# A selective scan over two images: image 0 reads its states out by C products summed in pairs, image 1 keeps transposed states

## The chip, the core and the metric

The kernel runs on one core of a Trainium2 chip. The metric is the device time of one execution in microseconds; before the change, seven executions have a median of 7278.53 us (7260.23 to 7296.72). Engine names are those of the profile: PE is TensorE (PEld its weight loads), DVE is VectorE, ACT is ScalarE, POOL is GpSimd, SP is SyncE, which here only issues DMAs.

## What is computed

The program is a two-layer network on 2 images of 128 channels and 64 x 64 positions, in float32. Layer 0 is a deformable convolution with four branches and a mixture of 8 experts; layer 1 is a Mamba-like mixer and a second mixture of experts. The change is in the mixer's selective scan, for 256 channels `d` (two halves of 128 partitions), 16 states `n` and 4096 positions `l` of each image:

```python
dA = jnp.exp(jnp.einsum('bdl,dn->lbdn', delta, A))
dBu = jnp.einsum('bdl,bnl,bdl->lbdn', delta, Bm, x)
def step(s, inp):
    a, bu, c = inp
    s = a * s + bu
    return (s, jnp.einsum('bdn,bn->bd', s, c))
_, ys = lax.scan(step, jnp.zeros((b, DI, DS), x.dtype), (dA, dBu, Ct))
y = jnp.transpose(ys, (1, 2, 0)) + x * D[None, :, None]
out = jnp.einsum('md,bdl->blm', out_proj_w, y * silu(z))
```

Per state the values of all positions are one recurrence; the readout multiplies state `n` by row `n` of C and sums over the 16 states.

## The kernel before

**Stages.** Up to about 5448 us the deformable convolution of both images runs, paced by gathers on POOL; beside image 1's sampling, image 0 goes through the rest of layer 0 and the mixer's convolutions. From 5448 to 7020 us the scan runs: image 0 first, then image 1. Beside image 0's scan the program does image 1's remaining work (`after(1)`: fusing the branches, L842 to L899; the experts' groups, `L0Ffn.group`; the mixer's convolutions, `L1Conv.convs`). Beside image 1's scan there is nothing but the scan's own preparation. After 7020 us comes the last mixture of experts.

**Units.** `L1Conv.scan` cuts each image into 8 chunks of 512 positions. A chunk has 32 units, one for each half and state; a unit is one recurrence over 128 partitions and 512 positions, so there are 256 units per image. The order of instructions on every engine is the order in which this Python loop emits them; each engine runs its own queue in order and waits on semaphores. For unit `u` the loop emits:

- SP: the B row of a unit six ahead (`fetch`, L1598), read from DRAM and spread over 128 partitions (tile `bcb`, 8 buffers).
- DVE: the scan of `u` (L1668): `h = da * state + db` from PSUM tile `da` and SBUF tile `db` into SBUF tile `h` (3 buffers).
- POOL: `db` of `u+3` (`drive`, L1580; 4 buffers), and the copy of the last column of `h` of `u-1` into `state` for the next chunk (L1677).
- ACT: `da` of `u+2`, an exponential into PSUM (`decay`, L1587; 2 buffers).
- PE: four 128 x 128 transposes of `h` of `u-1` into PSUM tile `ht` (`turn`, by the helper on L120; 2 buffers), so that positions lie on partitions and C is a scalar for each partition.
- DVE and ACT: `weigh` of `u-2`: C times `ht` into SBUF tile `w`. For image 0, DVE takes two of the four 128-column blocks in one instruction (L1614) and ACT the other two (L1616); for image 1, DVE one and ACT three.
- PE: four transposes of `w` of `u-3` back, accumulated over the 16 states in PSUM tile `py` (`add`, L1625), which an identity-like product with D (L1622) has started. After the 16th state, DVE multiplies `py` into the gate `zc` (L1637), and `project` multiplies by the output weights (L1710).

Between units the loop takes two steps of `prepare` (the next chunk: convolution taps, `x_proj`, `delta`, `du`; L1470 to L1548) and steps of `after(1)` worth one unit of credit, so how much of the other work stands beside each unit is fixed by the program.

**PSUM.** Eight banks: `da` 2, `ht` 2, `py` 1, and 3 (`scm`) for everything else.

Of the kernel before, what the change touches and what calls it, by code (L numbers as in the profile page):

```python
# [10 lines left out]
F32 = mybir.dt.float32  # L11
I32 = mybir.dt.int32
AF = mybir.ActivationFunctionType
ALU = mybir.AluOpType
# [5 lines left out]
P = 128  # L20
B = 2
C = 128
# [3 lines left out]
GT = 4  # L26
# [14 lines left out]
DS = 16  # L41
LC = 512
# [168 lines left out]
class L0Conv:  # L211
# [690 lines left out]
    def residual(self, b, g, keep, sp):  # L902

        nc, cut = self.env.nc, slice(g * 512, (g + 1) * 512)
        row = lambda name: sp.tile([P, 512], F32, name=name, tag="t", bufs=7)
        xr, fa, fn = row("xr"), row("fa"), row("fn")
        nc.sync.dma_start(out=xr, in_=self.env.d["x"][b, :, cut])
        nc.sync.dma_start(out=fa, in_=self.fd[b][:, cut])
        for _ in range(3):
            yield  # L910
        for py in range(2):
            nat = view(fn, py * W, [(2 * W, 4), (2, 32), (1, 2)])
            phases = view(fa, py * 256, [(32, 4), (1, 32), (P, 2)])
            nc.scalar.activation(nat, phases, AF.Relu, bias=keep[:, 1:2], scale=keep[:, 0:1])
        yield
        yield
        return xr, fn


class L0Ffn:  # L920
# [26 lines left out]
    def group(self, b, g, residual, norm, x2, sp, pp):  # L947
        env, nc = self.env, self.env.nc
        bank = lambda shape, name: pp.tile(shape, F32, name=name, tag="m")
        row = lambda name: sp.tile([P, GT, C], F32, name=name, tag="t", bufs=7)  # L950
        act = b > 0
        parts = yield from residual(b, g, sp)
        yield from self.take()
        pt = bank([P, GT, P], "pt")
# [127 lines left out]
AHEAD = 3  # L1082
BCB = 8

# [30 lines left out]
class L1Conv:  # L1115
# [315 lines left out]
    def taps(self, b, k, xc, xs, zz, sa, sp, bank, wk):  # L1431

        env, nc, halves = self.env, self.env.nc, range(2)
        if k == 0:
            self.wd = self.room().tile([P, 2, 4, P], F32, name="wd")
            for h in halves:
                for t in range(4):
                    nc.scalar.mul(self.wd[:, h, t, :], env.ident, self.w1[b][:, h, t : t + 1])
                yield
# [27 lines left out]
    def prepare(self, b, k, sp, pp, res):  # L1467
# [13 lines left out]
        def gap(n):  # L1481
            for _ in range(n):
                yield

        yield from gap(11)
        zz = sp.tile([P, 2, LC], F32, name="zc")
        nc.sync.dma_start(out=zz, in_=self.zsd[b].rearrange("(h p) l -> p h l", p=P)[:, :, l0 : l0 + LC])
# [3 lines left out]
        halves = range(2)  # L1491
        xs = sp.tile([P, 2, LC], F32, name="xs")
        if b:
            yield from self.taps(b, k, xc, xs, zz, sa, sp, bank, wk)
        else:
            yield from self.tap_sums(b, xc, xs, zz, sa, wk)
# [6 lines left out]
        nc.scalar.copy(xd, px)  # L1503
        bc = self.dp.tile([DS, LC], F32, name=f"bc{b}_{k}", tag=f"bc{b}_{k}")
        nc.sync.dma_start(out=bc, in_=xd[8 : 8 + DS, :])
        res.update(bc=bc)
        yield
        pt = bank([P, GT, 40], "pt")
        for j in range(GT):
            nc.tensor.transpose(pt[:, j, :], xd[:, j * P : (j + 1) * P], env.ident[0:40, 0:40])  # L1510
        yield
        ct = sp.tile([P, GT, DS], F32, name="ct")
        nc.scalar.copy(ct, pt[:, :, 8 + DS :])
        res.update(ct=ct)
        v = wk("v")
# [35 lines left out]
    def scan(self, sp, ps, pp, rest, ahead):  # L1551
# [18 lines left out]
        for _ in gen:  # L1570
            pass
        units = [(k, half, n) for k in range(B * NK) for half in range(2) for n in range(DS)]
        pieces, das, dbs, rows, hs, hts, ws = {0: res}, {}, {}, {}, {}, {}, {}

        def drive(u):

            if u < len(units):
                k, half, n = units[u]
                dbs[u] = sp.tile([P, LC], F32, name="db", bufs=AHEAD + 1)
                nc.gpsimd.tensor_tensor(dbs[u], pieces[k]["du"][:, half, :], rows.pop(u), ALU.mult)  # L1580

        def decay(u):
            if u < len(units):
                k, half, n = units[u]
                das[u] = ps.tile([P, LC], F32, name="da")
                dl = pieces[k]["dl"][:, half, :]
                nc.scalar.activation(das[u], dl, AF.Exp, scale=self.A[:, half, n : n + 1])  # L1587

        fetched = 0

        def fetch(u):
            nonlocal fetched
            while fetched <= min(u, len(units) - 1):
                k, half, n = units[fetched]
                if "bc" not in pieces.get(k, {}):
                    break
                rows[fetched] = sp.tile([P, LC], F32, name="bcb", bufs=BCB)
                nc.sync.dma_start(out=rows[fetched], in_=pieces[k]["bc"][n].partition_broadcast(P))  # L1598
                fetched += 1

        adds, py = deque(), {}

        def turn(u):
            hts[u] = ps.tile([P, GT, P], F32, name="ht")
            h = hs.pop(u)
            transpose4(nc, env.ident, hts[u], [h[:, j * P : (j + 1) * P] for j in range(GT)])

        def weigh(u):
            k, half, n = units[u]
            ct, ht = pieces[k]["ct"], hts.pop(u)  # L1610
            ws[u] = sp.tile([P, GT, P], F32, name="w", bufs=4)
            cut = 2 if k < NK else 1
            by = ct[:, 0:cut, n : n + 1].to_broadcast([P, cut, P])
            nc.vector.tensor_tensor(ws[u][:, 0:cut, :], ht[:, 0:cut, :], by, ALU.mult)  # L1614
            for j in range(cut, GT):
                nc.scalar.activation(ws[u][:, j, :], ht[:, j, :], AF.Copy, scale=ct[:, j, n : n + 1])  # L1616

        def add(u):
            k, half, n = units[u]
            if n == 0:  # L1620
                py[k] = ps.tile([P, LC], F32, name="py", bufs=1)
                nc.tensor.matmul(py[k], dg[:, half, :], pieces[k]["xs"][:, half, :], start=True, stop=False)  # L1622
            w = ws.pop(u)
            for j in range(GT):
                nc.tensor.matmul(  # L1625
                    py[k][:, j * P : (j + 1) * P],
                    w[:, j, :],
                    env.ident,
                    is_transpose=True,
                    start=False,  # L1630
                    stop=n == DS - 1 and j == GT - 1,
                )

        def gate(u):
            k, half, n = units[u]
            y = pieces[k]["zz"][:, half, :]
            nc.vector.tensor_tensor(y, y, py.pop(k), ALU.mult)  # L1637

# [3 lines left out]
        def flush(u):  # L1642
            while adds and adds[0][0] <= u:
                adds[0][1](adds.popleft()[2])

# [5 lines left out]
        side, keep, credit = Side(), None, 0  # L1651
        for u, (k, half, n) in enumerate(units):
            state = states[k // NK]
            if k and half == 0 and n == 5:
                side.todo.appendleft(project(k - 1))
            last = n == DS - 4 and half == 1
            if last and k == NK - 1:
                rest.drain()

            if k + 1 < B * NK and k + 1 not in pieces and (k != NK - 1 or not rest.todo):  # L1660
                gen, pieces[k + 1] = nxt(k + 1)
                side.add(gen)
            fetch(u + BCB - 2)
            if k >= NK and u % 24 == 12:
                ahead()

            hs[u] = sp.tile([P, LC], F32, name="h", bufs=3)
            nc.vector.tensor_tensor_scan(  # L1668
                hs[u], das.pop(u), dbs.pop(u), state[:, half, n : n + 1], ALU.mult, ALU.add
            )  # L1670
            if last:
                side.drain()
                fetch(u + BCB - 2)
            drive(u + AHEAD)

            if keep:
                nc.gpsimd.tensor_copy(*keep)  # L1677
            keep = state[:, half, n : n + 1], hs[u][:, LC - 1 : LC]
            decay(u + 2)
            if u:  # L1680
                turn(u - 1)
            if u > 1:
                weigh(u - 2)
            flush(u)
            adds.append((u + (4 if n == 0 else 3), add, u))
            if n == DS - 1:
                adds.append((u + 4, gate, u))

# [9 lines left out]
        for _ in project(B * NK - 1):  # L1698
            pass

    def project(self, b, k, ys, sp, pp):

        nc = self.env.nc
        xr = sp.tile([P, 2, LC], F32, name="xr", tag="wk", bufs=3)[:, 0, :].rearrange("p (j c) -> p j c", j=GT)
        nc.sync.dma_start(out=xr, in_=self.x2[b][:, k * GT : (k + 1) * GT, :])
# [18 lines left out]
    def run(self, after, ahead):  # L1724
# [4 lines left out]
        with (  # L1729
            tc.tile_pool(name="scs", bufs=2) as sp,  # L1730
            tc.tile_pool(name="scp", bufs=2, space=PSUM) as ps,
            tc.tile_pool(name="scm", bufs=3, space=PSUM) as pp,
        ):
            self.dtw = sp.tile([8, 256], F32, name="dtw", bufs=1)
            self.ow = sp.tile([P, 2, P], F32, name="ow", bufs=1)
# [249 lines left out]
def metaformer_kernel(ctx: ExitStack, tc: tile.TileContext, d: dict, out: bass.AP):  # L1985
# [6 lines left out]
    with tc.manual_schedule(engines={ET.PE, ET.DVE, ET.Activation, ET.Pool, ET.SP}), ExitStack() as l0:  # L1992
        mixer = L1Conv(env, dp, keep, x2, x3)
        mixer.room = lambda: ctx.enter_context(tc.tile_pool(name="wd", bufs=1, side="right"))

# [103 lines left out]
```

## Time and profile before

| | |
|---|---|
| median of 7 executions | 7278.53 us |
| profiled execution, its own time | 7272.12 us |
| its span | 7270.3 us |
| busy over the span: PE, DVE, ACT, POOL | 5068.8, 5803.2, 2261.2, 5084.2 us |
| mean granted TensorE clock | 0.86 of full speed |
| scan, image 0 (units 0 to 255) | 5448 to 6457 us |
| scan, image 1 (units 256 to 511) | 6457 to 7020 us |

The first scan instruction (L1668) starts at 5448.1 us and the last at 7018.4 us. The busy share of an engine over the whole span is a mean of stages with different limits, so the scan has to be read by itself. Durations in the groups are of single instructions; matmuls overlap each other, so a group's sum of matmul durations is more than the time that PE spends in it, while the busy time in a table by stage counts overlapped time once.

### The profile page before, as it was taken

How to read it: one execution, taken by the hardware profiler on the slowest of the kernel's cores; microseconds unless marked ns; L12 is line 12 of the kernel's file. 1: busy time of each engine (PE TensorE's matmuls, PEld its weight loads, DVE VectorE, ACT ScalarE, POOL GpSimd, SP SyncE). 2: the span in 40 equal slices, each digit the busy share in tenths (PEclk: the TensorE clock that was granted, in tenths of full speed). 3: DMA queues.
4: the chain of work that ended last, by engine and by line, in shares of the span. 5: the costliest groups of instructions: out<-in, count | busy, mean ns of one | idle time of the engine just before them, and what ended most of it. 6: DMA issues, size and time to landing. Idle time of an engine off the chain costs nothing.

```text
span 7270.3 us, 72120 instructions
## 1 busy us (share of the span) xinstructions
PE 5068.8 (70%) x22497; PEld 3193.2 (44%) x22497; DVE 5803.2 (80%) x6710; ACT 2261.2 (31%) x4642; POOL 5084.2 (70%) x5062
## 2 busy tenths in 40 slices
PE   4667777676666666766666776666547888867768
PEld 3444444444444442333333543443224567755544
DVE  5988888888888888898988888788866766677872
ACT  1211111111111111311111222121118777677860
POOL 4777777777777777777777777777765345567850
PEclk8888888988988987988888888888778888878889
DMA  7887777777777778877777888878765234544544
GB/s 219 272 285 224 236 221 232 221 234 222 229 224 225 230 218 267 304 238 227 234 233 219 256 252 241 249 244 248 226 185 182 79 106 130 142 149 155 169 138 162
DMA packets 667321, 1550.06 MB, mean 213 GB/s; under 512 B 181668, under 2 KB 230988, under 8 KB 666940
## 3 DMA queue, kind: packets, MB, share of 16 engines
q0 software_dynamic: 307200, 1006.88, 46.0%
q1 hardware_dynamic: 330812, 490.87, 21.3%
q10 hardware_dynamic: 28928, 47.70, 1.8%
q8 instruction: 182, 2.98, 0.2%
q14 instruction: 199, 1.63, 0.1%
HBM read 1436.70 MB, written 110.84 MB: 213 GB/s over the span
## 4 chain that ended last, share of the span: by engine, by line
PE 44%; issue 20%; DMA 10%; DVE 9%; POOL 8%; ACT 7%; SPq 2%; ACTq 0%; DVEq 0%; POOLq 0%
PE out L799 20%; POOL v L731 7%; PE pst L120 6%; DMA v<-table,idx 6%; PE po L428 5%; DVE v L772 2%; DVE h L1668 2%; ACT w L1616 2%; PE ps L1247 1%; PE ht L120 1%; PE ps L1234 1%; PE px L1028 1%; PE pfo L875 1%; PE py L1625 1%; DVE v L774 1%
## 5 line engine op out<-in xcount | busy, mean ns | idle before, releaser
L731 POOL DMA_INDIRECT v<-table,idx x3840 | 4085.3, 1064 | 1266.3 <-issue 996.7
L772 DVE TENSOR_TENSOR v<-v,pw 128x2048 f32<-128x2048 f32 x960 | 2192.1, 2283 | 615.3 <-DMA v<-table,idx 551.9
L799 PE MATMUL out<-st,regw 128*128 128x512 f32 x3840 | 2213.2, 707 | 95.3 <-ACT ys L813 87.2
L779 ACT COPY st<-pst 128x512 f32<-128x512 f32 x960 | 562.5, 586 | 3967.8 <-PE pst L120 3957.9
L120 PE MATMUL pst<-ident,v 128*128 128x128 f32 x3840 | 697.9, 312 | 1549.5 <-issue 1362.7
L120 PEld LDWEIGHTS pst<-ident,v 128*128 128x128 f32 x3840 | 479.4, 158 | 1984.0 <-issue 1752.0
L774 DVE TENSOR_TENSOR v<-v 128x1024 f32<-128x1024 f32 x960 | 1177.1, 1226 | 33.1
L799 PEld LDWEIGHTS out<-st,regw 128*128 128x128 f32 x3840 | 788.3, 228 | 702.3 <-issue 588.2
L1580 POOL TENSOR_TENSOR db<-du,bcb 128x512 f32<-128x512 f32 x512 | 672.1, 1313 | 509.6 <-DVE h L1668 384.5
L1668 DVE TENSOR_TENSOR_SCAN h<-da,state,db 128x512 f32<-128x512 f32 x512 | 651.9, 1273 | 85.3 <-ACT da L1587 50.8
L775 DVE TENSOR_TENSOR v<-v 128x512 f32<-128x512 f32 x960 | 664.2, 692 | 33.0
L120 PE MATMUL ht<-ident,h 128*128 128x128 f32 x2048 | 367.4, 309 | 233.0 <-ACT w L1616 206.6
L1587 ACT ACTIVATE da<-delta,w_A_log 128x512 f32<-128x512 f32 x512 | 360.2, 704 | 221.8 <-DVE h L1668 218.1
L120 PEld LDWEIGHTS ht<-ident,h 128*128 128x128 f32 x2048 | 265.0, 158 | 362.7 <-ACT w L1616 297.5
L1616 ACT ACTIVATE w<-ht,ct 128x128 f32<-128x128 f32 x1280 | 385.6, 373 | 19.9 <-DVE w L1614 19.7
L428 PEld LDWEIGHTS po<-wa,win 128*128 128x128 f32 x2112 | 319.3, 197 | 96.0 <-issue 96.0
L1614 DVE TENSOR_TENSOR w<-ht,ct 128x256 f32<-128x256 f32 (+1 forms) x512 | 173.4, 339 | 228.9 <-PE ht L120 226.5
L428 PE MATMUL po<-wa,win 128*128 128x147 f32 x2112 | 342.2, 294 | 0.0
L1625 PE MATMUL py<-ident,w 128*128 128x128 f32 x2048 | 341.4, 297 | 0.0
L1625 PEld LDWEIGHTS py<-ident,w 128*128 128x128 f32 x2048 | 276.1, 157 | 23.4 <-issue 23.1
L1234 PEld LDWEIGHTS ps<-ipw,hs 128*120 128x120 f32 x1408 | 180.8, 196 | 91.5 <-ACT X L1181 60.8
L1234 PE MATMUL ps<-ipw,hs 128*120 128x128 f32 x1408 | 188.8, 286 | 46.1 <-ACT X L1181 41.2
(327 smaller groups left out, 5189.3 us busy)
## 6 DMA issues: line engine op xcount, KB each, us to landing
bcb<-bc SPq DMA_DIRECT2D x512, 256.0 KB
regw<-in_regw SPq DMA_DIRECT2D x192, 640.0 KB
v<-table,idx POOLq DMA_INDIRECT x3840
yd<-ys ACTq DMA_DIRECT2D x128, 256.0 KB
yc<-yd SPq DMA_DIRECT2D x16, 2048.0 KB
wt<-in_weight SPq DMA_DIRECT2D x32, 1024.0 KB
tm<-pos SPq DMA_DIRECT2D x32, 720.0 KB
pos<-zero SPq DMA_DIRECT2D x48, 240.0 KB
```

Of the source, the lines that this page charges most:

```text
L120: nc.tensor.transpose(ps[:, j, :], s, ident)
L428: m()
L731: self.env.nc.gpsimd.indirect_dma_start(out=v[:, j, :], out_offset=None, in_=self.table[b], in_offset=bass.IndirectOffsetOnAxis(ap=idx[:, ...
L772: nc.vector.tensor_tensor(v4, v4, w, ALU.mult)
L774: nc.vector.tensor_tensor(up, up, v4[:, :, 2:4, :], ALU.add)
L775: nc.vector.tensor_tensor(v4[:, :, 0, :], v4[:, :, 0, :], v4[:, :, 1, :], ALU.add)
L779: nc.scalar.copy(st, pt.rearrange("p j t -> p (j t)"))
L799: nc.tensor.matmul(self.out[half], self.regw[t // CH][:, t % CH, half * P : (half + 1) * P], st, start=first, stop=last,)
L1580: nc.gpsimd.tensor_tensor(dbs[u], pieces[k]["du"][:, half, :], rows.pop(u), ALU.mult)
L1616: nc.scalar.activation(ws[u][:, j, :], ht[:, j, :], AF.Copy, scale=ct[:, j, n : n + 1])
L1625: nc.tensor.matmul(py[k][:, j * P : (j + 1) * P], w[:, j, :], env.ident, is_transpose=True, start=False, stop=n == DS - 1 and j == GT - 1,)
L1668: nc.vector.tensor_tensor_scan(hs[u], das.pop(u), dbs.pop(u), state[:, half, n : n + 1], ALU.mult, ALU.add)
```

## The change

For image 0 the transposes are gone. The units of image 0 now run over the states with the halves innermost, so that two successive units share one pair of rows. `fetch` loads the B row and the C row of one state together (tile `bcb`, 512 KB in a DMA, 5 buffers); for image 1 it loads the B rows of two successive states together. `prepare` stores C rows to DRAM too for image 0 (L1511), and leaves out the transposes that made C a column. The scan of image 0 is done in place in PSUM: `h` is `da`, which gets a third bank that image 1 uses for `py`. DVE then multiplies `h` by the spread C row into SBUF tile `sc` (L1701, 6 buffers). For every odd state, POOL adds the product of the state before it (`pair`, L1617), and PE adds that sum to `py` by one product with the identity over 512 columns (`identity`, L1621). Both halves' `py` are open at once (tag `x`, 2 banks, which image 1 uses for `ht`). The copy of the last column into `state` is on ACT for image 0, on POOL for image 1 as before.

Image 1 keeps its transposes, with DVE taking one block and ACT three, as before; `h` shares the six `sc` buffers, and `w` has 5 buffers. Around this, buffers are dealt out anew: a pool `scx` opens when image 1's preparation begins and holds `w`, `ct`, `wd`, every third `zc` and every second `xs` of image 1; image 0 has one `xs` buffer; `project` has its own `xr`; the preparation starts 5 steps earlier (`gap(6)`); the tile `t` of the experts' groups has 8 buffers.

```diff
@@ residual, L0Ffn.group
-        row = lambda name: sp.tile([P, GT, C], F32, name=name, tag="t", bufs=7)
+        row = lambda name: sp.tile([P, GT, C], F32, name=name, tag="t", bufs=8)
-BCB = 8
+BCB = 5
@@ prepare
-        yield from gap(11)
-        zz = sp.tile([P, 2, LC], F32, name="zc")
+        yield from gap(6)
+        own = self.own(b, sp)
+        third = b and k % 3 == 2
+        zz = (own if third else sp).tile([P, 2, LC], F32, name="zc", bufs=1 if third else 2)
...
-        bc = self.dp.tile([DS, LC], F32, name=f"bc{b}_{k}", tag=f"bc{b}_{k}")
-        nc.sync.dma_start(out=bc, in_=xd[8 : 8 + DS, :])
+        bc = self.dp.tile([DS, LC] if b else [DS, 2, LC], F32, name=f"bc{b}_{k}", tag=f"bc{b}_{k}")
+        if b:
+            nc.sync.dma_start(out=bc, in_=xd[8 : 8 + DS, :])
+        else:
+            for s in range(2):
+                nc.sync.dma_start(out=bc[:, s, :], in_=xd[8 + s * DS : 8 + (s + 1) * DS, :])
@@ scan
-        units = [(k, half, n) for k in range(B * NK) for half in range(2) for n in range(DS)]
+        units = [(k, n, half) for k in range(NK) for n in range(DS) for half in range(2)]
+        units += [(k, n, half) for k in range(NK, B * NK) for half in range(2) for n in range(DS)]
+        first = NK * 2 * DS
...
-                das[u] = ps.tile([P, LC], F32, name="da")
+                third = u < first and u % 3 == 2
+                das[u] = ps.tile([P, LC], F32, name="da", tag="y" if third else "da", bufs=1 if third else 2)
...
+                bcb[i] = sp.tile([P, 2, LC], F32, name="bcb", bufs=BCB)
+                nc.sync.dma_start(out=bcb[i], in_=(bc[n : n + 2] if k >= NK else bc[n]).partition_broadcast(P))
...
+        def pair(u):
+            nc.gpsimd.tensor_tensor(scs[u], scs.pop(u - 2), scs[u], ALU.add)
+        def identity(u):
+            nc.tensor.matmul(py[k, half], env.ident, scs.pop(u), start=False, stop=n == DS - 1)
...
-            hs[u] = sp.tile([P, LC], F32, name="h", bufs=3)
-            nc.vector.tensor_tensor_scan(
-                hs[u], das.pop(u), dbs.pop(u), state[:, half, n : n + 1], ALU.mult, ALU.add
-            )
+            s = das.pop(u)
+            h = s if u < first else sp.tile([P, LC], F32, name="h", tag="sc", bufs=6)
+            nc.vector.tensor_tensor_scan(h, s, dbs.pop(u), state[:, half, n : n + 1], ALU.mult, ALU.add)
...
-                nc.gpsimd.tensor_copy(*keep)
-            keep = state[:, half, n : n + 1], hs[u][:, LC - 1 : LC]
+                keep()
+            to, end = state[:, half, n : n + 1], h[:, LC - 1 : LC]
+            keep = functools.partial(nc.scalar.copy if u < first else nc.gpsimd.tensor_copy, to, end)
             decay(u + 2)
-            if u:
-                turn(u - 1)
-            if u > 1:
-                weigh(u - 2)
+            if pairs and pairs[0] < u:
+                pair(pairs.popleft())
+            if u < first:
+                scs[u] = sp.tile([P, LC], F32, name="sc", bufs=6)
+                nc.vector.tensor_tensor(scs[u], h, bcb[i][:, 1, :], ALU.mult)
...
+                if n % 2:
+                    pairs.append(u)
+                    adds.append((u + 3, identity, u))
```

## The prediction

> **What bounds the kernel now.** I read the stages first, since the change touches only the scan: the table of busy time by stretch, cut where the scan's chunks begin. The columns are the stretch in us from the start, its length, the busy time of PE, PEld, DVE, ACT and POOL with instruction counts, the granted clock, the DMA share and GB/s. The first five rows are image 0 (chunk 0; 1 and 2; 3 and 4; 5; 6 and 7), the last is image 1.
>
> ```profile
> core 0: us, PE busy (x) PEld busy (x) DVE busy (x) ACT busy (x) POOL busy (x), PEclk, DMA share, GB/s
> 5448.00:5570.00 122.00, 97.21 (x379) 54.21 (x380) 74.14 (x104) 102.98 (x182) 67.02 (x80) 0.88 0.63 218
> 5570.00:5893.00 323.00, 257.86 (x1254) 174.22 (x1253) 242.65 (x507) 245.40 (x551) 128.31 (x152) 0.84 0.26 83
> 5893.00:6121.00 228.00, 194.21 (x1562) 176.46 (x1561) 157.47 (x166) 157.41 (x351) 123.84 (x150) 0.87 0.50 139
> 6121.00:6260.00 139.00, 112.46 (x807) 93.66 (x805) 65.80 (x78) 96.72 (x192) 63.95 (x78) 0.83 0.47 120
> 6260.00:6457.00 197.00, 147.55 (x1030) 123.62 (x1031) 143.30 (x191) 132.88 (x291) 117.97 (x148) 0.81 0.51 150
> 6457.00:7020.00 563.00, 409.59 (x2406) 302.82 (x2405) 450.28 (x585) 461.90 (x1140) 454.69 (x565) 0.85 0.49 156
> ```
>
> Image 0 takes 1009 us, image 1 only 563 for the same 256 recurrences. Summed over the five rows, PE is busy 809 us (80%), ACT 735, DVE 683, POOL 501. Image 1 is another regime: DVE, ACT and POOL all near 80%. Next, what DVE waits for in image 0 (total us, times, longest), from the waits of 5448 to 6457:
>
> ```profile
> DVE w L1614 <- PE ht L120: 172.6, 87, 8.7
> DVE ws L1035 <- PE px L1028: 48.7, 17, 9.5
> DVE st L1326 <- DMA xst<-xsd: 22.8, 3, 11.5
> DVE h L1668 <- ACT da L1587: 21.4, 15, 5.1
> DVE h L1668 <- POOL state L1677: 11.2, 6, 3.3
> ```
>
> Of DVE's 326 idle us, 173 are `weigh` waiting for transposed states: PE's queue is full of other work, the transposes come late, and the next scan stands behind `weigh` on DVE. The scan is slowed by PE, not by its own inputs. Last the prices, the groups of the same stretch (count, busy us, mean ns, idle before):
>
> ```profile
> L1580 POOL TENSOR_TENSOR db<-du,bcb 128x512 f32<-128x512 f32 x260 | 334.8, 1288 | 436.4 <-DVE h L1668 322.5 <-DMA bcb<-bc 95.6 <-DVE w L1614 6.2
> L1668 DVE TENSOR_TENSOR_SCAN h<-da,state,db 128x512 f32<-128x512 f32 x257 | 327.3, 1273 | 36.8 <-ACT da L1587 21.4 <-POOL state L1677 11.2 <-POOL db L1580 3.9
> L1616 ACT ACTIVATE w<-ht,ct 128x128 f32<-128x128 f32 x506 | 156.5, 364 | 3.6 <-DVE w L1614 3.4
> L1614 DVE TENSOR_TENSOR w<-ht,ct 128x256 f32<-128x256 f32 x254 | 103.4, 407 | 173.4 <-PE ht L120 172.6
> L1677 POOL COPY state<-h 128x1 f32<-128x1 f32 x255 | 71.1, 279 | 0.0
> L1035 DVE TENSOR_TENSOR ws<-px,gate 128x512 f32<-128x512 f32 x32 | 22.0, 688 | 48.9 <-PE px L1028 48.7
> ```
>
> **The change, engine by engine, image 0.** *PE* loses 2 x 1024 transposes. Counted alone, the `ht` instructions occupy 184 us (19.7 + 49.3 + 42.9 + 23.8 + 48.2 over the five stretches) and those of L1625 171 us; both overlap with neighbours, so less than 355 leaves. It gains 128 identity products of 512 columns at 0.607 to 0.665 us (L1444 and L1028, same shape): 78 to 85. PE falls from 809 to between 530 and 640: no longer the bound.
>
> *ACT* loses 506 pieces of `weigh`, 156 us, and gains 256 copies of one column; the nearest row, an activation of 128x2, takes 0.202 us, so +52. From 735 to about 631.
>
> *POOL* loses 71 us of copies and gains 128 additions at 1.288: +165. From 501 to 595. It had 436 us of idle time before `db`, nearly all for DVE, so this is covered; uncovered it would cost 94.
>
> *DVE* loses 254 x 0.407 = 103 and gains 256 C products. These read one PSUM and one SBUF operand over 512 columns, like L1035: 256 x 0.688 = 176, so +72. Each waits for the scan just before it; the chain L772, L774, L775 shows 0.034 us of idle in such a step (33.1 us over 960): +9. The scan now writes PSUM instead of SBUF, in place. No row has that. Bounds: a copy into PSUM of 480 columns (L764, 0.658 us) costs per column what SBUF products do (L775, 0.692 for 512), so nothing; above, half a second pass over 512 columns of PSUM, 0.34 us a scan, 88 in all. I take nothing, by the copy, which is the only row that writes PSUM from DVE. Then there is POOL beside DVE:
>
> ```profile
> L1540 DVE SCALAR_TENSOR_TENSOR q<-delta,q x32: 1214/1983/2198, 5437.7 to 6955.4; 128x1024 f32<-128x1024 f32 x32
> L1637 DVE TENSOR_TENSOR zc<-zc,py x32: 671/682/689, 5526.9 to 7023.2; 128x512 f32<-128x512 f32 x32
> L1668 DVE TENSOR_TENSOR_SCAN h<-da,state,db x512: 1161/1273/1286, 5448.1 to 7018.4; 128x512 f32<-128x512 f32 x171
> ```
>
> (min/median/max ns.) The product of two SBUF operands stretches by up to 0.98 us; the two with a PSUM operand never do, though POOL works during more than half of them. So the C product stays at 0.69, and only the roughly 128 two-operand SBUF instructions of image 0 (`q`, `xs`, the experts' gates) pay more: POOL's share rises from 0.50 to about 0.64, half of a 1.29 us addition each, 128 x 0.14 x 0.64 = 11 us. [...] DVE in total: 683 + 72 + 9 + 11 = 775, or +11.5 per chunk; it becomes the busiest engine.
>
> **What is late next, stretch by stretch.** Chunk 0: ACT holds it (103 of 122 busy); less 20 of `weigh`, plus 6 of copies, 90; at the same share 107, taken as 110 with `da` waits. Chunks 1, 2: DVE 243 + 23 = 266; the `px` waits (48.7) halve because PE's queue is shorter, and 19 of small waits in that stretch stay: 309, taken 312. Chunks 3, 4: DVE waited 67 of its 71 idle us for `ht`; it has 157 + 23 = 180 of work and no other wait over 2: 200, at 90%. Chunk 5: DVE 77 plus 16 of waits is 93, but ACT keeps 82 at a share of 70% now: 115. Chunks 6, 7: DVE 166 plus waits that stay (`xst` 11, `xr` 9, small ones 8): 195. Sum 932 against 1009: -77.
>
> The rest: the row DMAs move the same bytes (2 rows for 2 units). Their buffers now come free by the C product of three units back instead of POOL, still six units ahead; behind such a wait SP holds the loads of `after(1)`, as it does today behind `db`. `zc` of the next chunk, issued 5 steps earlier, must wait on SP for `project` of the chunk before, with rows behind it for about 3 of those 6 units: covered, else some 5 us a chunk. PE's identity product waits for POOL's addition, emitted two units earlier; behind it stand `after(1)`'s matmuls, which ACT copies out. Six `h` buffers in image 1 take away DVE's wait for POOL's state copies (18.9 us there); POOL, at 81% there, gives half of it back: -9. The first two rows now arrive as one DMA of twice the size before the first scan: +2. Pools, `t` and `xr` buffers: nothing on a path in the trace; t's loads wait on SP, whose cover is six units of rows.
>
> Sum: -77 - 9 + 2 = -84. On the profiled execution's own 7272.1 that is 7188; its 7272.1 stands 6.4 below the median of the seven, so 7194 on the median.
>
> **The rivals.** *The bound only moves:* DVE becomes the busiest but reaches the same 79% that image 1's three engines reach. The busiest engine by stretch after (90, 266, 180, 88, 166) sums to 790; at 79% that is 1000, a gain of 9 plus some of image 1: 7262. For it: image 1 shows that share. Against: there DVE still waits for `ht` (53.5 us); in image 1's last chunk (6974 to 7018 us), which prepares nothing, DVE is busy 42.9 of 44 us. *The scan in PSUM costs:* if reading and writing one bank take turns, a scan gets up to a whole extra pass of 512 columns, 0.67 us, 172 in all, of which perhaps 60 fall into idle time: -84 + 112 = +28, and 7307. It decides from 0.33 us a scan on (84/256). Against: L764; for: no row shows DVE on PSUM both ways. *More:* waits shrink with PE's load, DVE runs at 90% (775/0.9 = 861) and image 1 gains all 19: -148 - 19, so 7112. That the change doesn't remove PE's transposes is no case: their instructions are gone from the program.
>
> **How the numbers follow.** Forecast 0.60; the bound only moves 0.18; scan in PSUM 0.12; more 0.10. The range reaches from halfway to "more" (7140) to just above "only moves" (7272), and leaves out most of the slow case and half of "more". A measurement of this kernel can tell about 0.2%, 15 us, from no change: faster by that holds the forecast, "more" and two thirds of "only moves", 0.82; the rest of that is "same", 0.06; slower 0.12.
>
> **What would show it.** After: DVE busy near 775 in image 0, PE under 640, no wait for `ht` before unit 256; the scan's row at 1.27 us and the C product's at 0.69; chunks 3, 4 shorten most. It is wrong if the scan takes over 1.6 us, if DVE waits for POOL's `db` or row DMAs by tens of us, or if image 0's end stays near 6457.

## The result, and the profile after

The changed kernel takes 7301.6 us (median of 18 runs, 7292.1 to 7323.0). Its ratio to the kernel before is 1.0035 (95% interval 1.0027 to 1.0043): slower by 0.35%, 23 us by the two medians and 25 by the ratio, where 84 us of gain were predicted. The profiled execution has a span of 7298.2 us, against 7270.3 before.

The table of busy time by stretch, after, has the columns of the prediction's first view; the last row is image 1, the five above it are chunk 0, chunks 1 and 2, 3 and 4, 5, 6 and 7 of image 0.

```profile
5440.00:5554.00 114.00, 83.94 (x170) 33.46 (x171) 83.88 (x105) 91.82 (x152) 80.23 (x64) 0.86 0.66 233
5554.00:5855.00 301.00, 210.21 (x786) 114.14 (x784) 263.42 (x505) 218.51 (x484) 154.62 (x121) 0.85 0.28 90
5855.00:6095.00 240.00, 192.01 (x1132) 149.85 (x1133) 177.91 (x167) 136.81 (x289) 149.85 (x120) 0.74 0.48 132
6095.00:6223.00 128.00, 102.45 (x559) 71.96 (x557) 77.27 (x79) 83.58 (x156) 78.27 (x62) 0.79 0.49 134
6223.00:6460.00 237.00, 143.37 (x579) 88.28 (x580) 167.23 (x190) 111.16 (x226) 142.86 (x116) 0.66 0.39 118
6460.00:7045.00 585.00, 416.95 (x2381) 304.90 (x2382) 443.60 (x583) 480.70 (x1148) 459.76 (x565) 0.84 0.44 152
```

The first scan starts 8 us earlier than before. Image 0 then takes 1019 us instead of 1009, image 1 586 instead of 563. Chunks 0 to 2 and 5 got shorter; chunks 3, 4, 6 and 7 got longer, and chunks 6 and 7 by 40 us. PE's busy time in image 0 fell only to 732 us, and the granted clock fell in the late stretches, to 0.74 and 0.66.

The prices, from the groups of image 0 after (count, busy us, mean ns, idle before):

```profile
L1686 DVE TENSOR_TENSOR_SCAN da<-da,state,db 128x512 f32<-128x512 f32 x256 | 328.4, 1283 | 102.0 <-ACT da L1598 90.1 <-ACT state L1693 7.8 <-POOL db L1590 3.9
...
L1621 PE MATMUL py<-sc,ident 128*128 128x512 f32 x253 | 180.1, 805 | 43.5 <-POOL sc L1617 43.5
...
L1701 DVE TENSOR_TENSOR sc<-da,bcb 128x512 f32<-128x512 f32 x256 | 177.0, 692 | 23.8 <-POOL sc L1617 2.2 <-PE py L1621 0.5
...
L1617 POOL TENSOR_TENSOR sc<-sc 128x512 f32<-128x512 f32 x127 | 169.3, 1333 | 0.0
...
L1693 ACT COPY state<-da 128x1 f32<-128x1 f32 x255 | 39.7, 156 | 113.8 <-DVE sc L1701 112.7 <-ACT fa L885 0.4
```

The scan in place in PSUM costs 1283 ns (1273 before) and the C product 692: what the prediction took. The wait for `ht` is gone. In its place DVE waits 90 us for `da` (21 before). Next, what else DVE waits for in image 0, from its waits:

```profile
DVE da L1686 <- ACT da L1598: 90.1, 39, 5.7
DVE st L1326 <- DMA xst<-xsd: 27.4, 5, 10.5
DVE xr L1759 <- DMA xr<-x: 25.7, 4, 9.3
```

(`xst` is read by a reduction in image 1's remaining work, `xr` holds the rows to which a chunk's projection is added.) The wait for `xst` was 23 us before, that for `xr` 9: nine loads now come late where four did. The waits of SP's queue show what stands ahead of them, first after, then before, in image 0:

```profile
SPq L1489 <- DVE zc L1654: 49.6, 6, 14.2
SPq L1489 <- PE po L1749: 46.7, 7, 10.0
```

```profile
SPq L1487 <- DVE zc L1637: 11.7, 1, 11.7
...
SPq L1487 <- PE po L1710: 6.4, 1, 6.4
```

Both lines are the load of the next chunk's `zc` (L1489 after, L1487 before). Before, SP stood there once, for 18 us, in the last chunk. After, it stands there in seven chunks, 96 us in all, until the gate and the projection have read the buffer's old content (5 to 21 us a chunk); rows, `xst`, `xr` and `sab` are queued behind. In image 1 the view to read is that of ACT's groups, the table loads, after:

```profile
L1598 ACT ACT_TABLE_LOAD x14 | 18.0, 1283 | 0.3
...
L1456 ACT ACT_TABLE_LOAD x7 | 9.0, 1283 | 0.0
...
L1459 ACT ACT_TABLE_LOAD x7 | 9.0, 1283 | 0.1
```

28 loads, where the kernel before has 14 (7 at L1456, 7 at the exponential). The two sigmoids of `taps` (L1456 and L1459) are one step apart in the preparation. Two steps run per unit. With a gap of 11 steps both fall behind the same unit; with 6 a unit's exponential falls between them, and in these seven preparations each change between sigmoid and exponential came with a table load of 1283 ns: four to a preparation, where there had been two.

The jobs below ran on several chips, on some of which the kernel before takes 7567 to 7626 us, so each ratio is to the kernel before on the same chip, and image 0 (start of unit 0 to start of unit 256) and image 1 (from there to the end of the last scan) are read in each run's own trace. Such a reading is of one execution. For the same code image 0 read 1009 and 1016 us before, 1019, 1030 and 1016 after (the last in the run with gap 7, which leaves image 0 as it is), and 980, 984 and 979 with gap 11: a difference of some 10 us says little unless the medians show it too.

### The profile page after: what moved, and what is told of

It reads as the page before. It is cut to its first block, busy times and chain, and to the rows that moved or that the text cites. A ratio compares the mean times of both kernels' runs of the same rounds, so it can differ in the third digit from the quotient of the medians.

```text
span 7298.2 us, 67466 instructions
## 1 busy us (share of the span) xinstructions
PE 5030.6 (69%) x20673; PEld 3048.3 (42%) x20673; DVE 5884.5 (81%) x6710; ACT 2187.4 (30%) x4394; POOL 5196.5 (71%) x4934
## 5 line engine op out<-in xcount | busy, mean ns | idle before, releaser
L799 PE MATMUL out<-st,regw 128*128 128x512 f32 x3840 | 2236.1, 714 | 88.7 <-ACT ys L813 81.8
L1686 DVE TENSOR_TENSOR_SCAN da<-da,state,db 128x512 f32<-128x512 f32 x256 | 328.4, 1283 | 102.0 <-ACT da L1598 90.1
L1598 ACT ACTIVATE da<-delta,w_A_log 128x512 f32<-128x512 f32 x512 | 360.1, 704 | 71.1 <-DVE h L1686 59.5
L1686 DVE TENSOR_TENSOR_SCAN h<-da,state,db 128x512 f32<-128x512 f32 x256 | 325.6, 1272 | 46.9 <-ACT da L1598 46.8
L120 PE MATMUL ht<-ident,h 128*128 128x128 f32 x1024 | 182.1, 305 | 168.0 <-ACT w L1635 157.7
L1247 PEld LDWEIGHTS ps<-tm,X 120*88 120x88 f32 x2048 | 220.6, 195 | 62.7 <-issue 26.5
L1635 ACT ACTIVATE w<-ht,ct 128x128 f32<-128x128 f32 x768 | 229.0, 386 | 24.6 <-DVE w L1633 24.6
L1247 PE MATMUL ps<-tm,X 120*88 120x48 f32 x2048 | 223.2, 285 | 18.8 <-ACT Y L1181 11.1
L120 PEld LDWEIGHTS ht<-ident,h 128*128 128x128 f32 x1024 | 125.6, 154 | 238.5 <-ACT w L1635 206.5
```

What stands on the lines that cost most here:

```text
L120: nc.tensor.transpose(ps[:, j, :], s, ident)
L799: nc.tensor.matmul(self.out[half], self.regw[t // CH][:, t % CH, half * P : (half + 1) * P], st, start=first, stop=last,)
L1247: nc.tensor.matmul(ps[:, c, :], X[:, ch + c0 + c, :], t[:, :, c0 % TG + c], start=True, stop=True)
L1686: nc.vector.tensor_tensor_scan(h, s, dbs.pop(u), state[:, half, n : n + 1], ALU.mult, ALU.add)
```

## The experiments

Three theories stood at the start for image 0: the lower clock makes PE's remaining work longer and the rest waits for it (T1); SP's queue is held up, so loads come late (T2); the state copy on ACT waits for the C product and holds ACT's queue (T3). The table loads were the theory for image 1.

### Gap 7 for image 1

```diff
-        yield from gap(6)
+        yield from gap(7 if b else 6)
```

> Only the preparation of image 1's chunks starts one step later than in the changed kernel (gap 7 instead of 6; image 0 keeps 6). In the changed kernel the two sigmoids of image 1's preparation (L1456 and L1459) have exponentials of the scan (L1598) between them, and the trace shows 28 function table loads of 1.283 us on ACT in image 1, against 14 before the change. Theory 'parity of the gap': with an odd gap the sigmoids stand next to each other again, 14 loads, ACT busy in image 1 falls by 14 x 1.283 = 18 us, the six even chunks fall from 75.1 to about 73 us and the kernel gets 14 to 20 us shorter than the changed kernel (7282 to 7288). Rival 'rows by pairs or the buffers cost image 1': the loads may go, but the chunks stay at 75 us and the time at 7302.

7276.8 us, ratio 1.0016 (1.0001 to 1.0030). ACT's table loads in image 1:

```profile
L1456 ACT ACT_TABLE_LOAD x7 | 9.0, 1283 | 0.0
...
L1598 ACT ACT_TABLE_LOAD x7 | 9.0, 1283 | 0.1
```

Image 1 takes 567 us instead of 586, chunks 9 to 14 72.2 on average instead of 75.1 (the loads at L1459 are gone, those at L1598 halved). One step of delay is worth 19 us: shown.

### Row DMAs on ACT's queue

```diff
-                nc.sync.dma_start(out=bcb[i], in_=(bc...
+                q = nc.sync if k >= NK else nc.scalar
+                q.dma_start(out=bcb[i], in_=(bc...
```

> Only the issue of image 0's row DMAs (bcb) moves from SP's queue to ACT's. On ACT they never wait longer than the exponential before them does, and on SP nothing stands before the loads xst, xr, zc, sab any more. Theory 'SP is held up by the rows' (T2): DVE's waits for xst and xr (27 and 32 us in image 0) and POOL's for rows (78 us) fall by more than half, chunks 5 to 7 get 15 to 30 us shorter together, about 7275 to 7287. Theories 'clock' (T1) and 'ACT is held by DVE' (T3): chunks 3 to 7 stay within 5 us, the time within 7296 to 7310 (ACT pays 128 issues).

7285.4 us, ratio 1.0030 (1.0015 to 1.0045), which can't be told from the changed kernel's 1.0035. Image 0 took 1003 us, 16 less than in the trace after and 12 less than with gap 7 on the same chip, and POOL's wait for rows fell from 78 to 39 us. But DVE still waited 31 us for `xst`, and SP still stood 95 us at `zc`. This run doesn't show what the rows had stood behind; SP's wait before each `zc` load does.

### PE kept busy with zero products

```diff
+        def warm(u):
+            k, n, half = units[u]
+            for j in range(2):
+                nc.tensor.matmul(py[k, half][:, j * 256 : (j + 1) * 256], env.zero[:, 0:P], dg..., start=False, stop=False)
...
+                adds.append((u + 3, warm, u))
```

> The changed kernel with PE kept busier in image 0: for each unit two more products with zero weights over 256 columns, accumulated into the open py, 154 us of PE at full clock over the 256 units; the values stay the same. Theory 'clock' (T1): the granted clock in chunks 3 to 7 rises from 0.74, 0.79 and 0.66 to 0.85 or more, the mean of the identity products falls from 805 to about 620 ns, and image 0 gets 20 to 40 us shorter (7262 to 7282) although PE has more to do. Rivals T2 and T3 (the clock falls because PE waits, and nothing hangs on it): the clock rises too, but image 0 stays within 5 us or gets longer, by up to 60 us if PE's queue is what the convolutions wait for.

7317.1 us, ratio 1.0064 (1.0045 to 1.0083). The clock rose to 0.91, 0.95 and 0.85 in chunks 3 to 7, and image 0 took 1035 us, 15 longer than in the trace after, 19 longer than with gap 7 on the same chip. As the rivals had it; but the products kept PE busy for 287 us in image 0, not the 154 expected, so the run can't tell what the clock alone is worth. A lighter dose follows below.

### No pair additions

```diff
-                if n % 2:
-                    pairs.append(u)
-                    adds.append((u + 3, identity, u))
...
+                adds.append((u + 3, identity, u))
...
```

> The changed kernel without POOL's pair additions: each of image 0's 256 C products goes into py by an identity product of its own, 128 more of them, 77 us of PE at full clock; POOL loses 128 x 1.33 = 170 us. Theory 'PE's queue waits for POOL' : PE's wait for sc (43.5 us, longest 18.5) goes, and image 0 gets 15 to 40 us shorter, most of it in chunks 6 and 7. Theory 'clock' (T1) expects 10 to 30 us too, but spread over chunks 3 to 7 with the clock at 0.85. Theories T2 and T3: image 0 within 8 us of 1019.

7302.0 us, ratio 1.0043 (1.0028 to 1.0057), image 0 1021 us (1016 with gap 7 on the same chip): no gain while `zc` holds SP. Whatever PE's wait for POOL's sums costs, it is not what made image 0 longer.

### Gap 11 for both images

```diff
-        yield from gap(6)
+        yield from gap(11)
```

> The changed kernel with the preparation started as late as before the change, for both images (gap 11 instead of 6). Theory 'SP is held by zc' (T2, made sharper): in the trace of the changed kernel SP's queue stands 5 to 22 us before each zc load of image 0 (L1489; 96 us in all, its buffer is read until the product and projection of the chunk before), where it stood 0.5 us before the change in all chunks but the last; rows, xst and xr stand behind it. With gap 11 this wait falls under 30 us, DVE's waits for xst and xr fall from 53 to about 30 us and POOL's for rows from 78 to under 40, image 0 and chunk 8 get 20 to 40 us shorter and image 1's chunks lose two table loads each (as in the run with gap 7: -17): 7250 to 7270 where the kernel before has 7278. Rivals T1 (clock) and T3 (ACT held by DVE): image 0 stays within 8 us of 1019, only image 1 gains, 7280 to 7290.

Ratio 0.9947 (0.9933 to 0.9960): faster than the kernel before. SP waits at most 0.2 us before any `zc` load of image 0. Image 0 took 984 us, chunks 9 to 14 72.8 on average. The clock in the late stretches stayed low (0.80, 0.73 and 0.70, after 0.74, 0.79 and 0.66), so the gain did not come from the clock.

### Gap 11 with row DMAs on ACT

The edits of the two runs together.

> As the run with gap 11, and image 0's row DMAs issued from ACT's queue. Alone, the move to ACT took 16 us from image 0. If that gain came from rows that stood behind zc on SP, nothing is left of it once zc doesn't wait: within 6 us of the run with gap 11. If SP's waits for row buffers (L1607 for the C product, 172 us in image 0) delay the other loads by themselves, another 10 to 20 us.

Ratio 0.9942 (0.9927 to 0.9957), image 0 985 us, against 984 on the same chip. Nothing is left of the gain that the move to ACT had shown in image 0, as expected if the rows had stood behind `zc`.

### Gap 11 with the state copies on DVE

```diff
-            keep = functools.partial(nc.scalar.copy if u < first else ...
+            keep = functools.partial(nc.vector.tensor_copy if u < first else ...
```

> As the run with gap 11, and image 0's copies of the last column into state on DVE instead of ACT. Theory 'ACT is held by DVE' (T3): ACT's waits in front of the copies (113 us) hold back conv copies and exponentials, DVE's wait for da (90 us) falls to under 45, image 0 gains 10 to 25 us although DVE pays 256 small copies (about 0.1 us each, 26 us). Rival: the exponential behind the copy waits for the same C product (its bank of PSUM), so ACT stands as long as before and image 0 gets 10 to 30 us longer by DVE's copies.

Ratio 0.9964 (0.9950 to 0.9977), image 0 990 us, 6 longer; by the medians on that chip 11 us longer. T3 falls: ACT stood 103 us before the copies for the C product; now it stands 206 us before the exponentials, which need the same bank, until DVE's copies have read it.

### Before, after and gap 11 on one chip

The kernels as they are, the run with gap 11 again, and gap 11 with the edit of the run without pairs.

> The kernel before, once more with a profile, so that the traces that are compared with it come from one chip. Expected: scan of image 0 about 1009 us, of image 1 about 563, SP standing about 0.5 us before each zc load but the last of image 0.

> The changed kernel, once more with a profile on the same chip as the others of this job. Expected: ratio to the kernel before 1.003, image 0 about 1019, image 1 about 586, SP standing 5 to 22 us before each zc load of image 0.

> The changed kernel with gap 11, on the same chip as the changed kernel and the kernel before. If the wait before zc and the table loads are what the change lost, the ratio to the kernel before is 0.993 to 0.996 again, some 55 to 65 us under the changed kernel: about 40 from image 0 and chunk 8, 17 from the table loads of image 1. If the first run with gap 11 owed its gain to its chip, the ratio is 0.999 to 1.002.

> The run with gap 11 without POOL's pair additions: each C product goes into py by an identity product of its own. With zc's wait gone, does the pair on POOL still cost anything? If PE's wait for POOL's sums (41 us, longest 7.8) holds up the convolutions on PE and ACT and so da, image 0 gets 8 to 20 us shorter than with gap 11 alone. If DVE and ACT set the pace there, it stays within 6 us, since PE has 77 us more to do.

| us | before | changed | gap 11 | gap 11, no pairs |
|---|---|---|---|---|
| ratio | 0.9993 (0.9982 to 1.0005) | 1.0046 (1.0032 to 1.0061) | 0.9961 (0.9948 to 0.9973) | 0.9952 (0.9937 to 0.9966) |
| median | 7273.9 | 7308.3 | 7250.9 | 7236.1 |
| image 0 | 1016 | 1030 | 980 | 970 |
| chunks 0 to 2 | 451 | 419 | 418 | 422 |
| chunks 3 to 7 | 566 | 611 | 562 | 548 |
| chunk 8 | 73.8 | 90.7 | 78.9 | 75.6 |
| image 1 | 564 | 589 | 563 | 559 |
| SP before `zc`, image 0 | 20 | 98 | 0.5 | 0.7 |

What DVE waits for in image 0, with gap 6 and then with gap 11, on this chip:

```profile
DVE da L1686 <- ACT da L1598: 94.1, 39, 7.2
DVE st L1326 <- DMA xst<-xsd: 28.7, 5, 11.4
DVE xr L1759 <- DMA xr<-x: 25.9, 4, 9.5
```

```profile
DVE da L1686 <- ACT da L1598: 85.2, 36, 5.0
...
DVE st L1326 <- DMA xst<-xsd: 15.8, 3, 6.6
...
DVE xr L1759 <- DMA xr<-x: 7.5, 2, 6.6
```

The waits for these two loads fall by 31 us, of the 50 by which image 0 gets shorter. The gap was worth 57 us by the medians. The traces give 50 in image 0 and 26 in image 1, less 21, since the first scan of the changed kernel started at 5433 us and that of gap 11 at 5454. (On the three chips where the kernel before takes about 7275 us, the scans of the kernels with gap 6 in image 0 began between 5430 and 5441, those of gap 11 and of the kernel before between 5448 and 5454; this earlier start was not taken apart.)

### Zero products at gap 11

```diff
+            nc.tensor.matmul(py[k, half][:, 0:256], env.zero[:, 0:P], dg..., start=False, stop=False)
...
+                adds.append((u + 3, warm, u))
```

> Gap 11 with the pairs kept, and for each unit of image 0 one product with zero weights over 256 columns, accumulated into the open py: 77 us of PE at full clock, as much as the 128 identity products that the run without pairs adds; the values stay the same. Theory 'clock' (T1): the granted clock of chunks 3 to 7 rises from 0.69-0.78 to 0.83 or more, the identity products fall from 0.80 us towards 0.65, and image 0 gets 7 to 14 us shorter than with gap 11 alone, the gain of the run without pairs. Rival 'PE waits for POOL's pair': the clock rises, image 0 stays within 4 us of gap 11 or gets longer.

> The run with gap 11 and no pairs again, on the chip of the run with zero products: image 0 8 to 14 us shorter than gap 11 with pairs, ratio to the kernel before 0.993 to 0.9955.

> The run with gap 11 and pairs again, as the neighbour of the other two on one chip: ratio to the kernel before 0.9945 to 0.9965, image 0 about 980 us, image 1 about 563.

Ratios in that order: 0.9956 (0.9942 to 0.9970), 0.9933 (0.9919 to 0.9946), 0.9956 (0.9940 to 0.9971); image 0 995, 974 and 979 us. The stretches of chunks 3 and 4, 5, 6 and 7, first of gap 11, then with zero products (PE, PEld, DVE, ACT, POOL, clock):

```profile
6151.00:6368.00 217.00, 174.77 (x1121) 135.29 (x1122) 180.82 (x165) 135.90 (x287) 152.17 (x118) 0.79 0.52 145
6368.00:6504.00 136.00, 113.89 (x569) 79.78 (x568) 78.23 (x80) 84.70 (x158) 80.56 (x63) 0.69 0.45 127
6504.00:6708.00 204.00, 131.28 (x578) 79.47 (x578) 167.45 (x189) 108.11 (x224) 144.97 (x116) 0.68 0.44 137
```

```profile
6159.00:6384.00 225.00, 185.50 (x1238) 147.77 (x1239) 182.17 (x168) 136.15 (x287) 152.93 (x119) 0.89 0.50 141
6384.00:6516.00 132.00, 117.21 (x644) 85.21 (x643) 78.09 (x79) 84.85 (x159) 80.31 (x63) 0.80 0.45 130
6516.00:6723.00 207.00, 147.81 (x706) 99.45 (x706) 168.46 (x190) 108.28 (x224) 144.69 (x115) 0.80 0.43 136
```

The zero products, over the same time:

```profile
L1625 PE MATMUL py<-dg,zero 128*128 128x256 f32 x512 | 176.3, 438 | 0.0
```

The clock rises by 0.10 to 0.12 and the identity products fall from 802 to 689 ns, as T1 had it, but nothing is gained: image 0 is 16 us longer in the trace (only chunk 5 is 4 us shorter), the medians stand 6 us apart and the ratios are the same. The dose was over twice the 77 us expected, so what a higher clock is worth without the products that make it stays open. About the same clock from useful work, without pairs (0.81 to 0.88), gives 5 us of image 0 here and 10 on the other chip, 17 and 15 by the medians; there 128 additions leave POOL as well. The clock is not what made the changed kernel slower than the kernel before: gap 11 undoes that with the clock still low. Its part in what gap 11 leaves is not shown.

### Without the sum, without the C products

Gap 11; the second run has both edits. Both leave terms of the sum out and were executed once, so only their traces are read.

```diff
-                if n % 2:
-                    pairs.append(u)
+                if n == DS - 1:
                     adds.append((u + 3, identity, u))
...
@@ the second run
-                scs[u] = ...
-                nc.vector.tensor_tensor(scs[u], h, bcb[i][:, 1, :], ALU.mult)
+                if n == DS - 1:
+                    scs[u] = ...
+                    nc.vector.tensor_tensor(scs[u], h, bcb[i][:, 1, :], ALU.mult)
```

> Gap 11, and image 0's sum over the states is left out: no pair additions, and of 128 identity products only the 16 of the last state. If PE's queue (identity products at 0.8 us, 100 us of PE, and their waits for POOL) holds the shortfall, image 0 falls from 980 to 930 to 950 us. If DVE with ACT's exponentials holds it, image 0 stays above 965.

> As the run before it, and image 0's C products are left out too, except those of the last state: 240 of 256, 240 x 0.69 = 166 us of DVE. If DVE sets the pace in all chunks, image 0 falls by 110 us or more against the run before it, spread evenly. If the chain of matmuls on PE and copies on ACT of the mixer's convolutions sets it, chunks 3 to 7 fall by less than 40 us together and chunks 1 and 2 by most of the rest.

Image 0 took 956 us (between the two cases expected) and then 901, chunks 3 to 7 548 and 510, chunks 1 and 2 295 and 282. The row of chunk 5 in the one and in the other:

```profile
6410.00:6541.00 131.00, 101.85 (x533) 76.89 (x531) 77.34 (x80) 84.28 (x158) 57.13 (x45) 0.63 0.45 132
```

```profile
6382.00:6514.00 132.00, 102.54 (x528) 77.86 (x526) 56.42 (x49) 83.50 (x157) 59.50 (x45) 0.61 0.46 130
```

166 us of DVE's work bring only 55: chunks 3 to 7 fall by 39, chunks 1 and 2 by 13 of the rest, as the case of the convolutions had it. In chunk 5, where DVE falls from 77 to 56, nothing. DVE does not set the pace there, nor does the sum. What is left is PE's and ACT's work on image 1's convolutions and the preparation, neither of them full (102 and 84 of 131 us); that this work sets the pace is argued, not shown.

### No pairs, products one unit later

```diff
-                adds.append((u + 3, identity, u))
+                adds.append((u + 4, identity, u))
...
-                    adds.append((u + 4, gate, k, half, (k, half)))
+                    adds.append((u + 5, gate, k, half, (k, half)))
```

> Gap 11 without pairs, and the identity product of a unit stands one unit later in PE's queue (u+4 instead of u+3), the product with the gate too. PE then waits less for the C product (19 us in image 0 without pairs and gap 6). If that wait holds convolutions and so ACT's exponentials, image 0 gets 4 to 10 us shorter than without pairs alone (970 to 974): ratio to the kernel before about 0.993. If not, it stays within 3 us.

Ratio 0.9932 (0.9912 to 0.9953), image 0 980 us. The run without pairs, on another chip, had 0.9933 and 974 us: no gain that can be told.

### Gap 6 with three `zc` buffers

```diff
-... name="zc", bufs=1 if third else 2)
+... name="zc", bufs=1 if third else 3)
```

with seven `t` buffers and five `sc` buffers to make room.

> The changed kernel with its gap of 6 and three zc buffers instead of two; to make room, t has 7 buffers (as before the change) and the C products 5 instead of 6. If SP's wait for the zc buffer is the cause, SP stands under 10 us before zc in image 0 (98 with two buffers), image 0 falls from 1019-1030 to 980-995, chunk 8 by 8 to 12, and the double table loads of image 1 stay (chunks 9 to 14 at 75 us): ratio to the kernel before 0.997 to 0.9995. If the place of the other instructions is the cause, image 0 stays at 1015 or more and the ratio at 1.002 to 1.005.

Ratio 0.9993 (0.9981 to 1.0005). SP no longer waits before any `zc` load, image 0 takes 989 us, chunk 8 83, and image 1's chunks 9 to 14 stay at 75.3 with 28 table loads. With the instructions in their places, the wait for the buffer cost image 0 30 to 41 us of the changed kernel's 1019 and 1030; the whole kernel gains 31 to 39 us by the ratios. Gap 11 takes some 5 to 10 us more. In this run ACT still waits 19 us to overwrite `xs` (L1404), of which image 0 has one buffer, until PE's product with D (L1613) has read it; after the change it was 12.5 us, and neither the kernel before nor gap 11 shows this wait. So the earlier start met a second buffer; what that alone costs was not tested.

## Why the prediction was wrong, by its steps

**The prices were right.** C product 692 ns against 688, scan 1283 against 1273 (the rival "the scan in PSUM costs" needed 0.33 us a scan, it was 0.01), DVE busy 770 us in image 0 against 775, POOL 606 against 595, ACT 642 against 631. That rival had the sign right and the mechanism wrong. Chunks 0 to 2 came out at 415 us (422 forecast).

**"Covered, else some 5 us a chunk": failed.** The prediction saw that `zc`, issued 5 steps earlier, waits on SP for the projection of the chunk before, and named rows as what stands behind it. It set the price by the rows and called them covered. SP stood 5 to 21 us, where three units take about 12, and `xst` and `xr`, which DVE takes in order, stood behind it as well. Price: 30 to 41 us (third buffer) or 39 to 50 (gap 11) in image 0, and 5 to 12 in chunk 8. "Pools, `t` and `xr` buffers" it put at nothing; the single `xs` buffer, which it did not name, made ACT wait.

**A term that was not in the sum.** Five steps shift the preparation by two and a half units, and the half decides which instructions share a unit. In image 1 that put exponentials between the sigmoids: 14 table loads, 18 us, measured as 19. This alone took the forecast gain of 9 in image 1. Nor does gap 11 bring the 9: chunks 9 to 14 are 1 us shorter each than before, 6 in all, and chunk 8 takes 5 of them. DVE's wait for POOL's state copies (18.9 us) is gone there, but its wait for `ht` grew from 54 to 65, and 10 us of waiting for POOL's `xs` are new.

**PE's fall to 530 to 640: failed, by a count.** PE was busy 732 us in image 0, and 718 to 730 with gap 11. The prediction took each of 128 identity products at 0.607 to 0.665 us, the mean of the rows L1444 and L1028. First the row of L1444 before, then the identity products after (min/median/max ns):

```profile
L1444 PE MATMUL pc<-xc,wd 128*128 128x512 f32 x128 | 61.8, 607 | 0.0
```

```profile
L1621 PE MATMUL py<-sc,ident x256: 592/595/1222, 5464.4 to 6463.2; 128*128 128x512 f32 x128
```

The program issues 64 products on L1444 (8 chunks, 2 halves, 4 taps) and 128 on L1621: each shows as two records, so the mean was that of half a product. With two records each the same prices give 155 to 170 us for the sum, and PE 605 to 725. Measured were 180, at granted clocks of 0.66 to 0.86 by stretch; the rest, 10 to 25, is put down to the clock, an estimate, since no run changed the clock alone: with gap 11 the same 256 records took 181 us, and with zero products, where the clock of chunks 3 to 7 was 0.10 to 0.12 higher, 154. With gap 11 the records took about 0.8 us on average; in the first such trace 156 of the 256 took under 0.7 us and 94 over 1.05, from 0.592 to 1.223, the longest 2.07 times the shortest. The expectations of added products (77 and 154 us) have the same half count; 176 and 287 were measured. What the sum costs image 0 is bounded by the run without it, 23 to 28 us.

**"Chunks 3, 4: 180 of work: 200, at 90%", chunk 5 115, chunks 6, 7 195: failed, also without `zc`'s wait.** Gap 11 gives 562 us for chunks 3 to 7, the forecast was 510, before 566. The wait for `ht` (173 us) was subtracted as if nothing came next; with gap 11 DVE waits 85 us for `da`, where it waited 21 before. It waits for ACT's exponential, and ACT, before it gets there, for PE's convolutions (64 us at L1181 and L1186 in the first run with gap 11) and for DVE's C product (103 us in the same run). Taking away the sum gave 9 to 14 us in chunks 3 to 7 and 23 to 28 in all of image 0; only without C products do chunks 3 to 7 reach 510. What sets chunk 5 at 128 to 135 us in all these runs was not isolated: no run took convolutions or preparation away.

So of the 109 us between forecast and result, 35 to 62 go with SP's wait (image 0 and chunk 8; the third buffer gives the low end, gap 11 the high one), 18 to 19 are the table loads, and some 50 are the shortfall that gap 11 leaves in image 0 (979 to 984 us where 932 were forecast), less some 10 by which the scan began earlier. The first two are shown by runs that take them away; the cause of the third is open.

The version to keep is gap 11 without pairs: 7236 us where the kernel before takes 7277, and ratios of 0.9952 and 0.9933 on two chips. It is shorter than both kernels by more than the noise, though by less than 1%; the gain is in image 0, where the C products pay and the additions on POOL do not.

## What to carry to other kernels

A load that is issued earlier is a wait that is issued earlier (here SP stood 96 us before `zc`, where it had stood 18): before moving one up an in-order DMA queue, find when its buffer's last reader is done, and list every transfer queued behind, with the engine that takes it in order. A shift of an interleaved program by an odd number of steps changes who stands beside whom; look for table loads where functions alternate on ACT (in image 1, 28 loads of 1283 ns between sigmoids and exponentials, where there had been 14). And a wait that is removed is not subtracted, it is replaced by the next input in line, which the busy times of a stretch don't show; here 64 us at `da` came for the 173 removed. And before a row's mean is taken as the price of an operation, divide the row's count by the operations that the program issues: here one product was two records.

## What the runs showed of the hardware

The DVE scan that reads and writes one PSUM tile in place took 1283 ns over 128x512 on average, 10 ns more than the scan from PSUM to SBUF before (1273). The 128 float32 products with the identity over 512 columns (L1621 after) show as 256 records on PE, of 0.592 to 1.222 us. The granted clock went with PE's load in chunk 5 of the runs with gap 11: 0.69 with PE busy 114 of 136 us, 0.80 with zero products (117 of 132), 0.63 without the sum (102 of 131). The busy share alone doesn't set it: the kernel before had 0.83 there with 112 of 139. At the end of the scan before (6974 to 7018 us) 239 of PE's 259 records are 128 x 128 transposes, and the clock is 1.00. A clock of 0.80 instead of 0.68, made by 64 zero products (128 records), brought no time in chunks 6 and 7 (207 us against 204), their own time on PE included.
